# Zero-weight matmuls of 128 columns in the scan slots with little planned TensorE work

## The chip, the cores and the metric

The kernel runs on one core of one Trainium2 chip, as one program. The metric is device microseconds (us) for one execution. TensorE (PE), VectorE (DVE), ScalarE (ACT), GpSimd (POOL) and SyncE (SP) each work through an instruction list of their own and wait for one another through semaphores.

## The reference, cut to what matters

The input `x` is 16 images of 48x48 pixels with 96 channels. Two layers follow each other; each is a state-space block and then a quantized feed-forward block, both with a residual sum. The state-space block projects to 192 channels, convolves, and scans every image in four directions, with 16 states for every channel:

```python
# layer 0; layer 1 is alike, with a layer norm behind the scan
xs = cross_scan(silu(depthwise_conv(xc, conv_w, conv_b, 1)))
delta = softplus(dts @ dt_proj_w + dt_proj_b)
def step(h, inp):
    d_t, u_t, B_t, C_t = inp
    h = h * jnp.exp(d_t[..., None] * A) + (d_t * u_t)[..., None] * B_t[:, :, None, :]
    return (h, jnp.einsum('bkdn,bkn->bkd', h, C_t))
y = cross_merge(scan(step) + Ds * xs) * silu(z)
x = x + y @ out_proj_w.T + ...
x = x + ffn(norm(x))
```

## The kernel before, in words

The scans are the long part: 16 images by 2 layers give 32 scan phases. A phase has 288 steps (`STEPS`: two direction pairs, three chunks of 768 pixels, twelve row blocks and four state groups), so there are 9216 steps, and a step is one tile of 128 rows by 768 pixels. Each step passes through four engines:

- `decays` (L647, L651): ACT forms the decay factor `a` with an exponential, from `dl`, into PSUM. There are two such tiles.
- `added` (L656, L661): POOL multiplies `du` by `bs` for two steps at once, into one of eight `ring` tiles.
- `step` (L708): DVE runs the scan (L727). Then either DVE multiplies by `cs` (L729), or POOL does it later for two steps at once (`product`, L740); a running sum of planned microseconds in `self.load` decides which. ACT copies the last column to `carry` (L731).
- `folded` (L664): PE sums the states. A group of 16 steps has one PSUM tile `py` with two halves q (a pool with one buffer). At the group's first fold a matmul with `first` opens the sum in each half (L673); each fold then adds four matmuls of 32 output rows (L685), and the fold with g = 3 closes the sum. `stored` (L697, L700) has ACT copy `py` out.

Beside the scan of one image runs the other work of its neighbours: norms, projections, 3x3 convolutions as diagonal matmuls (L447), the gates, the output projections (L918, L948) and the feed-forward blocks. This work is written as generators. Each `yield` returns a planned weight, and the loop of `scans` (L754 to L784), which goes through the steps as slots, takes from the phase's generator (`todo`) as long as the weight given is below the phase's share. In a slot the order of emission is: loads, planned work, `stored`, `step`, `decays` of two steps ahead, `added` of four steps ahead, `product`, and at last the due folds. That order, written out by hand, is each engine's instruction list. Products of planned work go to `pst` tiles of 128x512 (`pst()`, two buffers), which ACT reads ("put") in a later stage of the pipeline `piped`, mostly one yield after the product.

So PE's list is a mixture of folds, which wait for DVE or POOL, and planned products, which wait for ACT to have freed a `pst` tile or to have written an input.

Of the kernel before, what the change touches and what calls it, by code (L numbers as in the profile page):

```python
# [13 lines left out]
F32 = mybir.dt.float32  # L14
# [19 lines left out]
ND = 32  # L34
NG = 4
GROUPS = NS // NG
STEPS = 2 * NCH * 12 * GROUPS
SPARE = 1.0


_P = np.arange(128)
# [7 lines left out]
class Pack:  # L49


    def __init__(self):
        self.at, self.n, self.parts = {}, 0, []
# [83 lines left out]
TQ = SUB // 128  # L137


class Net:  # L140
    def __init__(self, ctx, tc, wpack, at, b2, ffw):
        self.tc, self.nc = tc, tc.nc
        nc = self.nc
        pool = lambda name, **kw: ctx.enter_context(tc.tile_pool(name=name, **kw))
        self.const = pool("const", bufs=1)
# [42 lines left out]
            )  # L188
        self.ident16 = self.const.tile([128, 128], F16, name="ident16")
        nc.vector.tensor_copy(self.ident16, self.ident)  # L190
        self.ones16 = self.const.tile([128, 128], F16, name="ones16")
        nc.vector.memset(self.ones16, 0.0)
        nc.vector.memset(self.ones16[:1, :], 1.0)
# [34 lines left out]
        for v, name in (("g", "ong"), ("b", "onb")):  # L228
            for i, half in enumerate("ab"):
                n = (128, 64)[i]  # L230
                o = self.const.tile([128, DM], F32, name=f"ow{half}{v}")
# [357 lines left out]
    def scans(self, phases, rest):  # L589
# [3 lines left out]
        nc, tc = self.nc, self.tc  # L593
# [9 lines left out]
        total = [w for _, _, _, w in phases]  # L603
        given = [0.0] * len(phases)
        tiles = {w: {} for w in ("dl", "du", "b", "c")}
        firsts, cur, pys, ring = {}, {}, {}, {}
        folds, done = collections.deque(), []
        kept = {"carry": None, "before": None, "last": 0, "here": True, "product": None}

        def ready(f):  # L610
            assert f == 0 or todo[f - 1] is None, "what a scan reads is not written yet"
# [29 lines left out]
        def load_first(group):  # L641
            f, t, s, pair, c, j, i, g = steps[group * 4 * GROUPS]
            ready(f)
            firsts[group] = self.sw.tile([128, CH], F32, name="first", bufs=1)
            nc.sync.dma_start(firsts[group], s["u" if pair == 0 else "y"][j][:, c * CH : (c + 1) * CH])

        def decays(n):  # L647
            f, t, s, pair, c, j, i, g = steps[n]
            a = self.ps.tile([128, 2, 512], F32, name="a", tag="ps").rearrange("p q f -> p (q f)")[:, :CH]
            dl = tiles["dl"][n // 16, i // 2]  # L650
            nc.scalar.activation(a, dl[:, i % 2, :], AF.Exp, scale=rates[t][:, pair, j, i, g : g + 1])  # L651
            cur["a", n] = a
# [3 lines left out]
        def added(n):  # L656


            i = n % 4
            b = self.sw.tile([128, 2, CH], F32, name="ring", bufs=8)  # L660
            nc.gpsimd.tensor_tensor(b, tiles["du"][n // 16, i // 2], both(tiles["b"][n // 4]), ALU.mult)  # L661
            ring[n // 2] = b

        def folded(n, q):  # L664


            f, t, s, pair, c, j, i, g = steps[n]
            group = n // (4 * GROUPS)
            if (g, q) == (0, 0):
                pys[group] = self.psy.tile([128, 2, 512], F32, name="py")  # L670
            py = pys[group]
            if g == 0:
                nc.tensor.matmul(  # L673
                    py[:, q, :SUB],
                    lhsT=self.skip[t][:, j, :] if pair == 0 else self.ident,
                    rhs=firsts[group][:, q * SUB : (q + 1) * SUB],
                    start=True,
                    stop=False,
                )
                if q == 1:  # L680
                    del firsts[group]
                    if (group + 1) * 4 * GROUPS % STEPS:
                        load_first(group + 1)
            for k in range(4):
                nc.tensor.matmul(  # L685
                    py[32 * k : 32 * k + 32, q, :SUB],
                    lhsT=self.fold,
                    rhs=ring[(n + k) // 2][:, k % 2, q * SUB : (q + 1) * SUB],
                    start=False,
                    stop=(g == GROUPS - 1),  # L690
                )
            if q == 1:
                del ring[n // 2], ring[n // 2 + 1]
            if (g, q) == (GROUPS - 1, 1):
                done.append(group)

        def stored(group):  # L697
            f, t, s, pair, c, j, i, g = steps[group * 4 * GROUPS]
            yt = self.sw.tile([128, CH], F32, name="yt", bufs=1)
            nc.scalar.copy(sub(yt), pys.pop(group)[:, :, :SUB])  # L700
            to = s["y"][j][:, c * CH : (c + 1) * CH]
            if (pair, j) == (1, 1):
                for i in range(4):
                    nc.sync.dma_start(to.rearrange("(h r) f -> h r f", h=2)[:, 16 * i : 16 * i + 16], yt[32 * i : 32 * i + 32])
            else:
                nc.sync.dma_start(to, yt)

        def step(n):  # L708
            f, t, s, pair, c, j, i, g = steps[n]
            if (j, i, g) == (0, 0, 0):  # L710
                kept["before"] = kept["carry"] if c != (0, NCH - 1)[pair] else None
                kept["carry"] = self.sw.tile([128, 12 * GROUPS], F32, name="carry")
            way = (lambda ap: ap) if pair == 0 else (lambda ap: ap[:, ::-1])
            last = CH - 1 if pair == 0 else 0
            at = (4 * j + i) * GROUPS + g
            start = 0.0 if kept["before"] is None else kept["before"][:, at : at + 1]
            a, b, cc = cur.pop(("a", n)), ring[n // 2][:, n % 2, :], tiles["c"][n // 4]

            load = self.load
            if n % 2 == 0:  # L720
                load["gp"] = max(load["gp"], load["ve"] - 6.0)
                here = kept["here"] = load["gp"] + 2 * 3.42 > load["ve"] + 2 * 1.81 + SPARE
                load["gp"] += 3.42 if here else 2 * 3.42
                load["ve"] += 2 * 2.76 if here else 2 * 1.81
            here = kept["here"]
            h = a if here else b
            nc.vector.tensor_tensor_scan(way(h), way(a), way(b), start, ALU.mult, ALU.add)  # L727
            if here:
                nc.vector.tensor_tensor(b, h, cc, ALU.mult)  # L729
            if c != (NCH - 1, 0)[pair]:  # L730
                nc.scalar.copy(kept["carry"][:, at : at + 1], h[:, last : last + 1])  # L731
            kept["last"] = max(kept["last"], n + (1 if here else 4))
            if n % 4 == 3:
                at = max(n + 2, kept["last"])
                folds.extend([(at, n - 3, 0), (at + 1, n - 3, 1)])

        def product(n):

            b = ring[n // 2]
            nc.gpsimd.tensor_tensor(b, b, both(tiles["c"][n // 4]), ALU.mult)  # L740
# [13 lines left out]
        for n in range(-10, len(steps) + 10):  # L754
            for load, of_what in loads.pop(n, ()):
                load(*of_what)
            if (n + STEPS - EARLY) % STEPS == 0 and 0 <= n // STEPS + 1 < len(todo):
                ready(n // STEPS + 1)
                next(todo[n // STEPS + 1])
            if 0 <= n < len(steps):  # L760
                f = n // STEPS
                share = (n % STEPS + 1 - START) / (END - START)
                here = 0
                while todo[f] is not None and (share >= 1 or given[f] < total[f] * share - (here > 0)):
                    w = next(todo[f], "end")
                    if w == "end":
                        todo[f] = None
                    else:
                        given[f] += w
                        here += w  # L770
            if done:
                stored(done.pop())
            if 0 <= n < len(steps):
                step(n)
            if 0 <= n + 2 < len(steps):
                decays(n + 2)
            if n % 2 == 0 and 0 <= n + 4 < len(steps):
                added(n + 4)
            if n % 2 == 1:
                if kept["product"] is not None:  # L780
                    product(kept["product"])
                kept["product"] = n - 1 if 0 <= n < len(steps) and not kept["here"] else None
            while folds and folds[0][0] <= n and not (done and folds[0][1] % (4 * GROUPS) == 0):
                folded(*folds.popleft()[1:])  # L784
        assert not (folds or done or pys or loads)
        self.alone = True
        for _ in rest:
# [459 lines left out]
```

## Time and profile before

| | |
|---|---|
| time, median of 3 runs | 25081.68 us (25062.27 to 25085.71) |
| profiled execution: its own time | 25084.31 us |
| profiled execution: its span, first to last instruction | 25082.5 us |
| mean granted TensorE clock | 0.788 |
| PE busy, of which the weight load row | 16821.3 us (67%), PEld 7108.9 us (28%) |
| DVE busy | 22225.7 us (89%) |
| POOL busy | 22715.5 us (91%) |
| ACT busy | 15229.2 us (61%) |
| matmul records | 70912 |
| DMA | 5011.40 MB, 61.4% of the 16 engines' time on SyncE's queue |

A matmul of float32 operands stands in the trace as two records, each with a weight load: the program has 37472 matmuls, and the profile 70912 records. "PEclk" is the share of full TensorE clock that the throttle granted. In this trace it is either 1.0 or 0.5, in stretches that are multiples of 3.413 us. A row of a waits view reads: engine, what it was about to run, "<-", what it waited for, and then microseconds in total, number of times, and the longest. A row of groups reads: line, engine, operation, output <- inputs, shape, count, then busy time, mean ns of one, and idle time before them.

### The profile page before, as it was taken

How to read it: one execution, taken by the hardware profiler on the slowest of the kernel's cores; microseconds unless marked ns; L12 is line 12 of the kernel's file. 1: busy time of each engine (PE TensorE's matmuls, PEld its weight loads, DVE VectorE, ACT ScalarE, POOL GpSimd, SP SyncE). 2: the span in 40 equal slices, each digit the busy share in tenths (PEclk: the TensorE clock that was granted, in tenths of full speed). 3: DMA queues.
4: the chain of work that ended last, by engine and by line, in shares of the span. 5: the costliest groups of instructions: out<-in, count | busy, mean ns of one | idle time of the engine just before them, and what ended most of it. 6: DMA issues, size and time to landing. Idle time of an engine off the chain costs nothing. (4 is left out here: it accounts for less than half of the span.)

```text
span 25082.5 us, 233858 instructions
## 1 busy us (share of the span) xinstructions
PE 16821.3 (67%) x70912; PEld 7108.9 (28%) x70912; DVE 22225.7 (89%) x15758; ACT 15229.2 (61%) x26690; POOL 22715.5 (91%) x7372
## 2 busy tenths in 40 slices
PE   5667667666677666776666766667666676667765
PEld 2223223222232222332222322223222232223322
DVE  6888989888998898988998889998899888999887
ACT  4566656666556665666655666666666566666654
POOL 6999999999999899998999989999899998999997
PEclk7888778877788777887778877788777887778876
DMA  5666666665666666666666666566665666666664
GB/s 180 206 201 203 192 201 212 205 208 189 200 207 205 204 196 197 202 209 202 203 193 201 209 202 208 187 202 210 202 213 191 194 205 203 214 199 193 203 207 133
DMA packets 1898962, 5011.40 MB, mean 200 GB/s; under 512 B 348000, under 2 KB 348000, under 8 KB 1879008
## 3 DMA queue, kind: packets, MB, share of 16 engines
q1 hardware_dynamic: 1820576, 4952.35, 61.4%
q10 hardware_dynamic: 77120, 44.09, 0.6%
q8 instruction: 560, 9.18, 0.2%
q14 instruction: 706, 5.78, 0.1%
HBM read 4104.27 MB, written 891.22 MB: 199 GB/s over the span
## 5 line engine op out<-in xcount | busy, mean ns | idle before, releaser
L661 POOL TENSOR_TENSOR ring<-du,bs 128x1536 f32<-128x1536 f32 x4608 | 15768.7, 3445 | 761.7 <-DMA bs<-bc 394.4
L651 ACT ACTIVATE a<-dl,l_a 128x768 f32<-128x768 f32 x9216 | 8313.8, 904 | 3102.0 <-DVE ring L729 2263.9
L727 DVE TENSOR_TENSOR_SCAN a<-a,carry,ring 128x768 f32<-128x768 f32 x4054 | 7352.1, 1814 | 747.0 <-ACT a L651 679.1
L685 PE MATMUL py<-ring,fold_sb 128*32 128x384 f32 x36864 | 5212.3, 605 | 3041.7 <-POOL ring L740 2504.8
L740 POOL TENSOR_TENSOR ring<-ring,cs 128x1536 f32<-128x1536 f32 x1652 | 5687.4, 3443 | 823.3 <-issue 663.2
L729 DVE TENSOR_TENSOR ring<-a,cs 128x768 f32<-128x768 f32 x5912 | 5661.3, 958 | 463.5 <-DMA cs<-bc 71.0
L727 DVE TENSOR_TENSOR_SCAN ring<-a,carry,ring 128x768 f32<-128x768 f32 x2090 | 3691.8, 1801 | 362.0 <-ACT a L651 301.7
L727 DVE TENSOR_TENSOR_SCAN a<-a,ring 128x768 f32<-128x768 f32 x1858 | 3255.3, 1752 | 430.4 <-ACT a L651 367.9
L685 PEld LDWEIGHTS py<-ring,fold_sb 128*32 128x32 f32 x36864 | 1062.4, 122 | 6659.8 <-POOL ring L740 2964.4
L731 ACT COPY carry<-a 128x1 f32<-128x1 f32 x3778 | 600.1, 159 | 3723.5 <-DVE ring L729 3713.8
L727 DVE TENSOR_TENSOR_SCAN ring<-a,ring 128x768 f32<-128x768 f32 x1214 | 2069.8, 1740 | 193.0 <-ACT a L651 142.1
L339 PE MATMUL pst<-dts,wpack_sb 128*128 128x384 f32 x2304 | 1213.1, 665 | 1243.6 <-ACT dl L571 1217.2
L447 PE MATMUL pst<-e,dg 128*128 128x384 f32 x5184 | 1782.9, 493 | 0.0
L553 POOL TENSOR_TENSOR du<-dl,u 128x768 f32<-128x768 f32 x576 | 1042.6, 1820 | 564.2 <-DMA dd<-du 356.6
L447 PE MATMUL pst<-wxa,dg 128*128 128x384 f32 x3456 | 1220.9, 504 | 64.0 <-DMA dg<-taps_l1a 41.9
L447 PEld LDWEIGHTS pst<-e,dg 128*128 128x128 f32 x5184 | 945.9, 189 | 841.2 <-issue 214.4
L339 PE MATMUL pst<-xt,wpack_sb 96*128 96x384 f32 (+1 forms) x1536 | 766.5, 635 | 477.6 <-ACT wxb L482 261.2
L339 PEld LDWEIGHTS pst<-dts,wpack_sb 128*128 128x128 f32 x2304 | 512.6, 247 | 1929.3 <-ACT dl L571 1534.4
L673 PE MATMUL py<-first,l_skip 128*128 128x384 f32 x1152 | 655.5, 659 | 549.5 <-ACT yt L700 484.7
L339 PE MATMUL pst<-u,wpack_sb 128*128 128x384 f32 x2304 | 886.3, 531 | 190.8 <-ACT u L518 81.9
L673 PE MATMUL py<-first,ident 128*128 128x384 f32 x1152 | 631.8, 638 | 516.7 <-ACT yt L700 492.8
L339 PE MATMUL pst<-y,centre 128*128 128x384 f32 (+1 forms) x1536 | 819.3, 690 | 120.3 <-ACT y L969 114.8
(171 smaller groups left out, 17496.5 us busy)
## 6 DMA issues: line engine op xcount, KB each, us to landing
du<-dd SPq DMA_DIRECT2D x1536, 384.0 KB
dl<-dd SPq DMA_DIRECT2D x1536, 384.0 KB
bs<-bc SPq DMA_DIRECT2D x1536, 384.0 KB
cs<-bc SPq DMA_DIRECT2D x1536, 384.0 KB
du<-dd SPq DMA_DIRECT2D x1536, 192.0 KB
dl<-dd SPq DMA_DIRECT2D x1536, 192.0 KB
bs<-bc SPq DMA_DIRECT2D x1536, 192.0 KB
cs<-bc SPq DMA_DIRECT2D x1536, 192.0 KB
```

Source lines behind the costliest of these rows:

```text
L339: nc.tensor.matmul(img(o[: w.shape[1], :SUB]), lhsT=w, rhs=y, start=(k == 0), stop=(k == len(terms) - 1))
L447: nc.tensor.matmul(img(o[:, :SUB]), lhsT=dg[:n, k, :], rhs=img(p[:n], PW)[:, PQ * q + i : PQ * q + i + PQ, j : j + HW], start=(k == 0), st ...
L553: nc.gpsimd.tensor_tensor(du, dl[:, cs], u[j][:, cs], ALU.mult)
L651: nc.scalar.activation(a, dl[:, i % 2, :], AF.Exp, scale=rates[t][:, pair, j, i, g : g + 1])
L661: nc.gpsimd.tensor_tensor(b, tiles["du"][n // 16, i // 2], both(tiles["b"][n // 4]), ALU.mult)
L673: nc.tensor.matmul(py[:, q, :SUB], lhsT=self.skip[t][:, j, :] if pair == 0 else self.ident, rhs=firsts[group][:, q * SUB : (q + 1) * SUB], ...
L685: nc.tensor.matmul(py[32 * k : 32 * k + 32, q, :SUB], lhsT=self.fold, rhs=ring[(n + k) // 2][:, k % 2, q * SUB : (q + 1) * SUB], start=Fal ...
L727: nc.vector.tensor_tensor_scan(way(h), way(a), way(b), start, ALU.mult, ALU.add)
L729: nc.vector.tensor_tensor(b, h, cc, ALU.mult)
L731: nc.scalar.copy(kept["carry"][:, at : at + 1], h[:, last : last + 1])
L740: nc.gpsimd.tensor_tensor(b, b, both(tiles["c"][n // 4]), ALU.mult)
```

## The change

The builder keeps account of the TensorE time that it emits in a slot, and at the slot's end it adds matmuls with zero weights until the account reaches 1.2.

- A wrapper around `nc.tensor` (`Timed`, `Core`) adds to `spent` for every matmul: columns of the output times 4 for float32 (1 for other types), divided by 2400, and by 3 for the folds with 32 output rows.
- `spent` is set to zero in each slot ahead of the planned work.
- Behind the slot's folds `filled` forms n, the rounded (1.2 - spent) / 0.213, and emits n matmuls of 128 columns with the stationary operand `zero` (128x128, all zeros) and `ident` as the moving one.
- Where a sum of `py` is open (from the opening matmul to the fold with g = 3) they are added into its first 128 columns. Where none is open and the slot had no planned work, they go to a new `pst` tile named "fill". Otherwise none is emitted.
- One memset on DVE makes `zero`.

```diff
+FILL = 1.2
+class Timed:
...
+    def matmul(self, out, lhsT, rhs, **kw):
+        n = 1
+        for k in out.shape[1:]:
+            n *= k
+        self.spent[0] += n * (4 if rhs.dtype == F32 else 1) / 2400 / (3 if out.shape[0] == ND else 1)
+        return self.engine.matmul(out, lhsT=lhsT, rhs=rhs, **kw)
...
+        self.zero = self.const.tile([128, 128], F32, name="zero")
+        nc.vector.memset(self.zero, 0.0)
...
+            if g == 0:
+                begun[q] = py[:, q]
+            elif g == GROUPS - 1:
+                del begun[q]
             for k in range(4):
                 nc.tensor.matmul(
                     py[32 * k : 32 * k + 32, q, :SUB],
...
+        def filled(busy):
+
+            n = int((FILL - self.spent[0]) / 0.213 + 0.5)
+            if n <= 0:
+                return
+            if begun:
+                o, start = next(iter(begun.values()))[:, :128], False
+            elif not busy:
+                o, start = self.pst("fill")[:, :128], True
+            else:
+                return
+            for _ in range(n):
+                nc.tensor.matmul(o, lhsT=self.zero, rhs=self.ident, start=start, stop=start)
...
+            self.spent[0], here = 0.0, 0
             if 0 <= n < len(steps):
                 f = n // STEPS
                 share = (n % STEPS + 1 - START) / (END - START)
-                here = 0
...
             while folds and folds[0][0] <= n and not (done and folds[0][1] % (4 * GROUPS) == 0):
                 folded(*folds.popleft()[1:])
+            filled(here > 0)
```

More of the change, by code (lines that the diff above doesn't have):

```diff
@@ L137, with __init__, __getattr__ @@
 TQ = SUB // 128
+class Timed:
+    def __init__(self, engine, spent):
+        self.engine, self.spent = engine, spent
+    def __getattr__(self, name):
+        return getattr(self.engine, name)
+    def matmul(self, out, lhsT, rhs, **kw):
[4 more added lines that the diff above has]
+        return self.engine.matmul(out, lhsT=lhsT, rhs=rhs, **kw)
+class Core:
+    def __init__(self, nc, spent):
+        self.nc, self.tensor = nc, Timed(nc.tensor, spent)
+    def __getattr__(self, name):
+        return getattr(self.nc, name)
 class Net:
     def __init__(self, ctx, tc, wpack, at, b2, ffw):
-        self.tc, self.nc = tc, tc.nc
+        self.spent = [0.0]
+        self.tc, self.nc = tc, Core(tc.nc, self.spent)
         nc = self.nc
@@ L605, in scans @@
         tiles = {w: {} for w in ("dl", "du", "b", "c")}
-        firsts, cur, pys, ring = {}, {}, {}, {}
+        firsts, cur, pys, ring, begun = {}, {}, {}, {}, {}
         folds, done = collections.deque(), []
```

## The prediction

> **What bounds the kernel now.** I read the page's busy rows first, then the waits of DVE, ACT and PE, then PE's stretches at half clock.
>
> ```profile
> PE 16821.3 (67%) x70912; PEld 7108.9 (28%) x70912; DVE 22225.7 (89%) x15758; ACT 15229.2 (61%) x26690; POOL 22715.5 (91%) x7372
> ...
> PEclk7888778877788777887778877788777887778876
> ```
>
> DVE and POOL are near full, ACT and PE are not: the work of DVE and POOL is the floor, and PE counts only where it makes them wait. The page also says that the clock is low in every slice, 0.788 in the mean.
>
> ```profile
> DVE a L727 <- ACT a L651: 1047.0, 612, 7.4
> DVE ring L727 <- ACT a L651: 443.8, 281, 5.4
> ...
> ACT yt L700 <- PE py L685: 333.5, 194, 8.9
> ACT xs L953 <- PE pst L918: 289.1, 141, 3.9
> ACT y L969 <- PE pst L339: 259.2, 86, 5.0
> ...
> PE py L685 <- POOL ring L740: 2504.8, 452, 20.4
> PE pst L339 <- ACT dl L571: 1217.2, 217, 18.3
> ```
>
> The first two rows are how PE can reach the end: DVE's scan waits 1490.8 us (1047.0 + 443.8) for ACT's exponential, and ACT, which takes its list in order, may be late because a copy ahead of the exponential waited for PE. ACT's rows that wait for PE (sixteen of 30 us and more; three are shown) sum to 2045 us. Going through the idle times behind those 1490.8 us, and looking in the six us before each for an ACT wait for PE, I find 840 us so explained; in 244 of the 840 the granted clock was a half. The last two rows say why PE itself is late: its next matmul waits for POOL or ACT, up to 20 us, with planned work queued behind it.
>
> **What the clock follows.** Two pairs of neighbouring windows of the clock's 3.413 us grid (stretch, length, then busy time of PE, PEld, DVE, ACT and POOL, granted clock, DMA share, GB/s):
>
> ```profile
> 2619.35:2622.77 3.42, 3.42 (x24) 3.25 (x23) 3.42 (x4) 2.77 (x6) 3.42 (x2) 1.00 0.02 7
> 2622.77:2626.18 3.41, 3.41 (x13) 3.02 (x13) 3.32 (x4) 1.67 (x5) 3.41 (x2) 0.50 0.72 223
> ...
> 2639.83:2643.25 3.42, 1.35 (x6) 0.30 (x2) 3.38 (x3) 1.82 (x3) 3.42 (x2) 1.00 0.00 1
> 2643.25:2646.66 3.41, 1.65 (x6) 0.58 (x10) 2.32 (x3) 3.36 (x6) 3.41 (x2) 0.50 0.56 174
> ```
>
> In the third PE works 1.35 us of 3.42, and the next is at half clock. In the first PE is "busy" throughout, but with one-column matmuls (L984) whose time is weight loading; the next is at half clock too. So I counted the time in which columns stream, over all windows of the trace. Of 910 windows at full clock with columns streaming for under 0.37 of the window, 1% were followed by full clock; of 3309 above, 99%. At half clock the bound is 0.75 (1% below, 93% above): the same number of columns.
>
> **The change part by part.**
>
> *What is added.* The built program has 16103 fills behind 3964 of 9236 slots, mostly six (1959 slots, nothing planned) or two (1704 slots, one fold). The order on ACT, POOL and SP is unchanged, and DVE has one memset more at the start; that memset I cost at nothing, since DVE waits there for the weights' DMA. Nothing is removed.
>
> *What one fill costs.* No row has it. Two near ones:
>
> ```profile
> L447 PE MATMUL pst<-e,dg 128*128 128x384 f32 x5184 | 1782.9, 493 | 0.0
> ...
> L918 PE MATMUL pst<-wpack_sb,y 128*128 128x96 f32 x1152 | 199.5, 303 | 0.0
> ```
>
> Busy time over count is 0.344 us a record for the convolution at 384 columns, nearly all at full clock; a third of it, twice, is 0.229 us a fill. The 96-column row with the same weight load, over both clocks, gives 0.173 a record, 0.346 a fill. I take 0.28: 4.5 ms in all (3.7 to 5.6), against 8261 us in which PE is idle now.
>
> *What it does to the clock.* A slot is 2.72 us (25082.5 / 9216). Six fills stream for 1.28 us, 47% of it; two fills and a fold (0.64 us) for 39%. Paced by slots, that would be just over 0.37. But PE isn't paced by slots: fills carry no wait (215 wait for ACT and 118 for PE, the rest for nothing), so PE runs them as soon as it reaches them, then stands at the next fold or product as before. In PE's list they lie in 2723 runs, up to 26 or 32 long. They shorten idle times without pacing them, and where PE stands over one window behind a fold it still falls to half clock. I estimate 0.86 from laying the fills into the record (each starts when the matmul ahead of it ends): a third of the half-clock time goes.
>
> *The gain.* A third of the 244 us at half clock, halved: 41 us. Bounds: 0, and 146 us if all of PE's half-clock work (5949 us of its busy time) ran at full clock, by the rate below (2974 x 0.12 x 0.41). I take 50.
>
> *The loss.* Each fill stands ahead of the next fold or product in PE's list. 8593 stand ahead of folds, which wait now in any case (3041.7 us idle before L685, for POOL's product mostly): cover, and I cost them at nothing; without that cover they would come under the same rate. 7510 stand ahead of planned products (6558) or opening matmuls (952): 2.1 ms at 0.28. Now PE's 16821 us make ACT wait 2045, 0.12 per us, and 0.41 of that (840 of 2045) reaches DVE: 2.1 ms x 0.12 x 0.41 = 103 us. Lower end: 0, if all fall into idle time. Upper end: in the laid record, matmuls that stay where the trace shows them waiting but yield to the fills come 630 us later, in sum, than ACT's reads could bear (0.224 us a fill at full clock, 0.43 at half), 1131 us at 0.3 and 0.5; by 0.41 that is 258 or 464 us. Most is at the gates of the last stage (L830) and the third projection of the branch (L881, L883), where ACT follows close behind PE. I take 170, between the mean rate and the lower laid value, since DVE's own delays move the releases too.
>
> *Two small things.* A fill into a `pst` tile waits until ACT has read the tile's last product, and the next product then waits for the fill; products waiting for PE rise from 97 to 294, at 0.1 to 0.3 us each below 60 us, in the range. Inside a sum, two fills between a group's last two folds make `yt` some 0.5 us later where ACT waits for it (194 times, 333.5 us): counted in the loss.
>
> **Sum.** 25084.3 (the profiled execution's own time, 2.6 us above the median) + 170 - 50 = 25204, rounded 25205 us: slower by 0.5%.
>
> [...] The first window above is busy without a gap and loses the clock. [...]
>
> **The rivals.**
>
> *The fills fall into idle time* (27%). For it: 8261 us idle against 4.5 ms, the one slot of slack between a product and its read, and a DVE that waits for ACT more than for anything else. Against it: PE's lateness comes in bursts after a long wait, and the runs stand in just those bursts. Then only the gain is left, 50 to 146 us: 24980. This ends faster; it decides where a run's delay (6 x 0.28 = 1.7 us) stays below the 2.72 us of a slot.
>
> *Gain and loss cancel* (15%): each below 100 us, 25085, within 0.2%. That is about what a measurement of this kernel can tell from no change.
>
> *The clock doesn't move* (7%), because bursts leave the idle windows as they are or zero operands don't count as activity: the loss without the gain, 25255.
>
> *Backlog* (7%). In the last stage a slot pair has 2.56 us of centring products, folds and up to eight fills; at half clock eight fills take 3.4 of the pair's 5.4 us, PE no longer catches up, and 464 us are lost: 25550.
>
> **How the numbers follow.** My forecast, loss over gain, has 44%: 25205, of 25140 to 25400. Slower by over 0.2%: 44 + 7 + 7 = 58%; same 15%; faster 27%. The range runs from 24940 (the idle rival with nearly all of the gain) to 25480 (near the forecast's upper bound) and leaves out most of the backlog case and the best tail.
>
> **What would show it.** Right: a granted clock of 0.84 to 0.88, 16103 matmuls more (32206 records) at some 0.28 us, ACT's waits for PE up by some 400 us with L830 and L883 in front, and DVE's wait for ACT up by about 120. Wrong: ACT's waits for PE fall; then the fills were covered. A clock near 0.79 means the third rival; a clock over 0.93 means that pacing holds, and the gain is larger than I bound it.

## The result, and the profile after

The changed kernel takes 25327.58 us (median of 4, 25316.15 to 25333.9) against 25071.97 (median of 4): a ratio of 1.0101, 95% interval 1.0086 to 1.0117, or 256 us more. The profiled execution has a span of 25321.1 us and a granted clock of 0.872, after 0.788. The same lines of the page as for before:

```profile
PE 20054.1 (79%) x103118; PEld 10736.0 (42%) x103118; DVE 22188.8 (88%) x15759; ACT 15234.3 (60%) x26690; POOL 22747.1 (90%) x7372
...
PEclk8888889888888888888888988889888898888888
```

DVE, ACT and POOL have the same work, and their operations take as long as before (the exponential 904 ns before and 903 now, the scan that starts from `carry` 1814 in both). PE has 32206 records more, and no slice of its clock is below eight tenths, after 23 of 40 before. Yet DVE, whose span less busy time was 2856.8 us, now stands idle for 3132.3, or 275 us more: all of the difference is waiting. The waits of DVE and ACT in the changed kernel (microseconds, times, longest; the lines of the code moved down by 29 to 48, L774 is the scan, L680 the exponential, L1017 the copy of the centred product that was L969, and L154 is the wrapper through which all matmuls but the transposes now pass):

```profile
DVE a L774 <- ACT a L680: 1158.4, 628, 8.7
DVE ring L774 <- ACT a L680: 464.8, 285, 5.2
DVE ring L774 <- ACT carry L778: 150.5, 63, 10.4
...
ACT y L1017 <- PE pst L154: 411.6, 86, 12.0
ACT yt L747 <- PE py L154: 389.5, 187, 10.1
ACT xs L1001 <- PE pst L154: 341.1, 141, 4.7
...
PE py L154 <- POOL ring L787: 1311.1, 360, 18.3
PE pst L154 <- ACT dl L600: 851.8, 191, 11.4
PE fill L154 <- ACT y L1017: 81.0, 16, 10.9
```

DVE waits for the exponential 1623.2 us, 132 more than before. Over all of its rows it waits for ACT 2331.5 us after 2066.4, 265 more: the exponential is only half of the growth, and the copies of `carry` (74 us) and the root ahead of the reciprocal (26) are most of the rest. ACT waits more for PE: its rows that name PE, all of them, sum to 2545 us after 2173. The greatest growth is not where PE waits longest, but in one row: the centred products, 259.2 us before and 411.6 now. PE's own waits for POOL and ACT have shrunk (the two greatest rows from 2504.8 and 1217.2 us to 1311.1 and 851.8): fills stand in what was idle time, of which 5267.0 us are left of 8261.2.

Where in the run is the time? The starts of the 9216 scans give each phase's length. Of every four phases, the two with the last and the first stages in their planned work became 15.0 and 11.3 us longer (six phases of each kind in the middle of the run), the two with the middle stage 4.5 us longer and 0.2 us shorter. And within the first two kinds it is the first 48 of 288 steps. The table gives the mean of 13 such phases, in us for eight steps each; the last three rows belong to runs told below.

| run | 0-8 | 8-16 | 16-24 | 24-32 | 32-40 | 40-48 | sum |
|---|---|---|---|---|---|---|---|
| before | 22.5 | 21.4 | 25.8 | 23.5 | 17.8 | 20.5 | 131.7 |
| changed | 22.6 | 23.2 | 31.3 | 26.8 | 17.8 | 24.9 | 146.6 |
| no fills in centring | 22.5 | 21.5 | 25.7 | 23.4 | 17.8 | 20.1 | 131.1 |
| plain operands, before | 22.7 | 19.3 | 20.9 | 19.9 | 17.9 | 23.3 | 124.0 |
| plain operands, fills | 22.7 | 19.3 | 21.1 | 22.2 | 19.5 | 25.8 | 130.7 |

Fifteen such phases by 14.9 us are 224 us of the 256. These steps are `centred`: the centring products of layer 1 (steps 8 to 32), then 36 one-column matmuls for the sums of squares (L984 before) and the reciprocal on DVE (about 32 to 48). PE's order of time there, before, and then in the changed kernel (start, length, what ran, and the idle time ahead of it):

```profile
6411.81 8.14 PE L339 MATMUL pst<-y,centre 128*128 128x384 f32 x16
6419.87 0.85 PE L685 MATMUL py<-ring,fold_sb 128*32 128x384 f32 x8
6423.58 8.14 PE L339 MATMUL pst<-y,centre 128*128 128x384 f32 x16 [2.85 <-ACT y L969]
6431.65 1.50 PE L685 MATMUL py<-ring,fold_sb 128*32 128x384 f32 x16
6435.86 9.48 PE L339 MATMUL pst<-y,centre 128*128 128x384 f32 x16 [2.72 <-ACT y L969]
```

```profile
6475.11 8.04 PE L154 MATMUL pst<-y,centre 128*128 128x384 f32 x16
6483.07 0.85 PE L154 MATMUL py<-ring,fold_sb 128*32 128x384 f32 x8
6483.86 4.29 PE L154 MATMUL py<-ident,zero 128*128 128x128 f32 x36
6487.98 8.04 PE L154 MATMUL pst<-y,centre 128*128 128x384 f32 x16
6495.94 0.85 PE L154 MATMUL py<-ring,fold_sb 128*32 128x384 f32 x8
6496.73 0.71 PE L154 MATMUL py<-ident,zero 128*128 128x128 f32 x4
6497.37 0.85 PE L154 MATMUL py<-ring,fold_sb 128*32 128x384 f32 x8
6500.94 2.93 PE L154 MATMUL fill<-ident,zero 128*128 128x128 f32 x12 [2.72 <-ACT y L1017]
6503.93 9.49 PE L154 MATMUL pst<-y,centre 128*128 128x384 f32 x16
```

A pair of product rows stands in one slot, and the next pair about four slots, 10.9 us, later. The pair takes PE 8.14 us, and folds 0.85 to 1.7: 1 to 2 us are free. The builder's account puts the pair at 5.12 us, all in one slot, sees empty slots behind it and orders fills there: 18 behind the first pair shown (4.29 us), and 2 and 6 behind the second (0.71 and 2.93 us). Behind the first pair PE works on without a gap and still falls behind: 12.9 us to the next pair. Behind the second it stands 2.72 us ahead of the fills that take a `pst` tile, which ACT has yet to read, and the next pair comes 16.0 us after. Before it was 11.8 and 12.3. ACT's copy waits behind PE:

```profile
6477.89 0.47 ACT L1017 COPY y<-pst 64x384 f32<-64x384 f32 x1 [6.94 <-PE pst L154]
6478.26 0.19 ACT L778 COPY carry<-ring 128x1 f32<-128x1 f32 x1
6478.35 0.90 ACT L680 ACTIVATE a<-dl,l_a 128x768 f32<-128x768 f32 x1
```

The exponential, for which DVE's next scans wait, stands two places behind that copy.

### The profile page after: what moved, and what is told of

The parts are those of the page before. It is cut to its first block, busy times and chain, and to the rows that moved or that the text cites. A ratio compares the mean times of both kernels' runs of the same rounds, so it can differ in the third digit from the quotient of the medians.

```text
span 25321.1 us, 298313 instructions
## 1 busy us (share of the span) xinstructions
PE 20054.1 (79%) x103118; PEld 10736.0 (42%) x103118; DVE 22188.8 (88%) x15759; ACT 15234.3 (60%) x26690; POOL 22747.1 (90%) x7372
## 5 line engine op out<-in xcount | busy, mean ns | idle before, releaser
L680 ACT ACTIVATE a<-dl,l_a 128x768 f32<-128x768 f32 x9216 | 8312.5, 903 | 3048.7 <-DVE ring L776 2222.1
L774 DVE TENSOR_TENSOR_SCAN a<-a,carry,ring 128x768 f32<-128x768 f32 x4054 | 7354.3, 1814 | 771.9 <-ACT a L680 693.5
L154 PE MATMUL py<-ring,fold_sb 128*32 128x384 f32 x36864 | 4797.2, 562 | 1493.0 <-POOL ring L787 1311.1
L154 PEld LDWEIGHTS py<-ident,zero 128*128 128x128 f32 x28894 | 3722.0, 204 | 1717.1 <-issue 1673.3
L154 PE MATMUL py<-ident,zero 128*128 128x128 f32 x28894 | 4164.2, 297 | 0.0
L774 DVE TENSOR_TENSOR_SCAN ring<-a,carry,ring 128x768 f32<-128x768 f32 x2090 | 3691.9, 1801 | 357.5 <-ACT a L680 299.2
L774 DVE TENSOR_TENSOR_SCAN a<-a,ring 128x768 f32<-128x768 f32 x1858 | 3255.6, 1752 | 543.8 <-ACT a L680 464.9
L154 PEld LDWEIGHTS py<-ring,fold_sb 128*32 128x32 f32 x36864 | 865.4, 115 | 4027.1 <-issue 1775.9
L774 DVE TENSOR_TENSOR_SCAN ring<-a,ring 128x768 f32<-128x768 f32 x1214 | 2071.1, 1741 | 262.1 <-ACT a L680 165.6
L154 PE MATMUL pst<-dts,wpack_sb 128*128 128x384 f32 x2304 | 1143.6, 633 | 859.1 <-ACT dl L600 851.8
L154 PE MATMUL pst<-e,dg 128*128 128x384 f32 x5184 | 1779.9, 493 | 0.0
L154 PEld LDWEIGHTS pst<-e,dg 128*128 128x128 f32 x5184 | 946.0, 189 | 823.0 <-issue 198.8
L154 PE MATMUL pst<-wxa,dg 128*128 128x384 f32 x3456 | 1197.6, 495 | 36.9 <-DMA dg<-taps_l1a 20.3
L154 PEld LDWEIGHTS pst<-dts,wpack_sb 128*128 128x128 f32 x2304 | 497.0, 240 | 1391.0 <-ACT dl L600 1130.4
L154 PE MATMUL pst<-u,wpack_sb 128*128 128x384 f32 x2304 | 855.9, 517 | 118.7 <-ACT u L547 50.4
L154 PE MATMUL pst<-xt,wpack_sb 96*128 96x384 f32 (+1 forms) x1536 | 681.6, 574 | 297.0 <-ACT wxb L511 184.1
L154 PE MATMUL py<-first,l_skip 128*128 128x384 f32 x1152 | 613.0, 620 | 336.7 <-ACT yt L747 307.4
```

The lines of the kernel that those rows point to most:

```text
L154: return self.engine.matmul(out, lhsT=lhsT, rhs=rhs, **kw)
```

## The experiments

Theory A: all of the loss is PE's overfilled list in the centring stage. The first rivals are B, the mean rate of the prediction (every fill ahead of planned work costs alike), and C, the fills that take a `pst` tile. Later ones are D, that the clock is worth nothing, and E, that fills hurt in the stage for another reason than PE's time. Each time stands beside the kernel before on the same chip.

**Without the fills of the centring stage.** The flag is true from `loaded_y` in `centred` to behind the reciprocal.

```diff
+        self.centring = True
...
-            if n <= 0:
+            if n <= 0 or self.centring:
```

> The fills of the centring stage are left out (1738 of 16103, 11%); the other 14365 stay. Theory A, backlog in the centring stage: its strided products take PE 8.04 us of every four slots (10.9 us), so that fills there overfill PE; all of the loss is there. The time falls by 200 to 260 us, to between 25050 and 25130, DVE's waits for ACT fall back to about 1490 us, and the granted clock stays near 0.865. Theory B, the mean rate of the prediction (every fill ahead of a planned product costs alike): some 11 to 15% of the loss goes, 25290, and ACT's waits for PE stay above 2450 us.

25092.36 us, ratio 1.0012 (1.0003 to 1.0021), at a clock of 0.868.

```profile
DVE a L775 <- ACT a L681: 1061.2, 621, 7.4
DVE ring L775 <- ACT a L681: 456.5, 284, 5.4
...
ACT y L1019 <- PE pst L154: 258.9, 86, 4.9
```

The centred copies wait for PE as long as in the kernel before. Theory A holds and B falls: 11% of the fills carry nine tenths of the loss, and the other 14365 together cost 26 us, net of what the clock gives. ACT's rows that name PE sum to 2326 us, 153 more than before, and DVE stands idle for 55 us more (2911.4).

**Only these.**

```diff
-            if n <= 0:
+            if n <= 0 or not self.centring:
```

> The complement: only the 1738 fills of the centring stage. Theory A: slower than before by 200 to 250 us, 25280 to 25320, though the clock stays near 0.79. Theory B: by 30 to 40 us, 25105 to 25115.

25310.92 us, ratio 1.0097 (1.0083 to 1.0110), clock 0.795. The complement gives 244 us: the loss is there, and the clock is hardly touched by it. Here ACT's waits for PE grow by 237 us (to 2410) and DVE's idle time by 240 (to 3096.7): all of the lateness arrives at DVE. Two lines of its waits, which are almost those of the changed kernel:

```profile
DVE a L775 <- ACT a L681: 1159.1, 613, 8.6
...
ACT y L1019 <- PE pst L154: 418.9, 86, 11.7
```

**No fills into a tile of their own.**

```diff
-            elif not busy:
-                o, start = self.pst("fill")[:, :128], True
             else:
                 return
```

> The 1656 fills that take a pst tile are left out; the 14447 into open sums stay. Theory C, the tile: a fill that takes one of two pst tiles waits for ACT, and the next product waits for the fill, so that double buffering is lost; the loss goes with the tile, 25090 to 25150. Theory A: the fills into open sums overfill PE in the centring stage (1528 of its 1738), and at most 60 us come back, 25260 to 25320.

25258.45 us, ratio 1.0076 (1.0062 to 1.0090). Some 65 us come back (0.25%), a little over A's bound and far from C's: C holds for that part alone. The tile counts for about a quarter of the loss: in the centring stage a fill takes the tile that ACT has yet to read (the wait of 2.72 us in the order of time above), and PE stands there. The first 48 steps of a phase fit that: 141.4 us here, after 146.6 in the changed kernel.

**All fills with one column.**

```diff
-                nc.tensor.matmul(o, lhsT=self.zero, rhs=self.ident, start=start, stop=start)
+                nc.tensor.matmul(o[:, :1], lhsT=self.zero, rhs=self.ident[:, :1], start=start, stop=start)
```

> All 16103 fills, of one column instead of 128: about the same time of PE each (two weight loads, 0.27 us at full clock by the one-column rows of before) but hardly a column streamed. By the count of windows of before, the clock then stays near 0.78. Theory A with a clock that is worth some 50 us: 25370 to 25400, slower than the changed kernel by the worth of the clock. If weight loads count for the clock: 0.87 and 25330 as in the changed kernel. If the clock is worth nothing: 25330 at a clock of 0.78.

25826.63 us, ratio 1.0304 (1.0289 to 1.0318), clock 0.764: slower than the changed kernel by 499 us, not by the expected 50. The direction and the clock are A's, the size was wrong tenfold. The page's first line shows PE busy for longer than in the changed kernel, and yet at the lower clock:

```profile
PE 22162.9 (86%) x103118; PEld 12355.1 (48%) x103118; DVE 22216.4 (86%) x15759; ACT 15227.6 (59%) x26690; POOL 22737.3 (88%) x7372
```

So more weight loading didn't raise the clock here (PEld 7108.9 us at 0.788 in the kernel before, 12355.1 at 0.764), and columns of zero weights did (10736.0 at 0.872 in the changed kernel). The size has the centring stage in it (160.8 us for 48 steps after 146.6); the next run but one takes that out.

**Fills in the sparse phases alone.**

```diff
+            if n <= 0 or self.centring:
...
-            filled(here > 0)
+            if n // STEPS % 4 in (0, 3):
+                filled(here > 0)
```

> Fills only in the phases whose planned work is that of a last and a first stage (two of every four, with little of it), and none in the centring stage: 8283 fills. With the centring stage left out those phases were 2.4 to 2.8 us shorter each than before, 16 of them, and the others longer by 1 to 4 us. Theory A with a clock that is worth something where PE has little to do: 25025 to 25045 beside a before of 25067, faster by 0.1 to 0.2%. Theory D, the clock is worth nothing and the phases moved by chance: 25060 to 25085.

25054.06 us, ratio 0.9998 (0.9989 to 1.0007), clock 0.835. No difference from before that can be measured: neither theory is confirmed.

**One column, none in the centring stage.** Both edits above together.

> As the run without fills in the centring stage (25092), but each fill is of one column. The same 14365 fills in the same places, hardly a column streamed. Theory A with a clock that pays for the queue time of the fills: outside the centring stage the one-column kernel was some 35 us longer in every four phases than the changed one, so about 25370, at a clock near 0.77. Theory D, clock worth nothing: 25090 to 25120 at a clock near 0.77.

25335.99 us, ratio 1.0110 (1.0095 to 1.0126), clock 0.770. With 128 columns the same list took 25092, at a clock of 0.868: 244 us of difference, where D expected 25090 to 25120, so D falls. The first line of both pages, and the rows of the fills into open sums, first with 128 columns and then with one:

```profile
PE 19664.4 (78%) x99642; PEld 10338.8 (41%) x99642; DVE 22186.0 (88%) x15759; ACT 15228.1 (61%) x26690; POOL 22738.7 (91%) x7372
...
L154 PE MATMUL py<-ident,zero 128*128 128x128 f32 x25838 | 3714.6, 296 | 0.0
```

```profile
PE 21505.3 (85%) x99642; PEld 11722.4 (46%) x99642; DVE 22195.6 (88%) x15759; ACT 15232.0 (60%) x26690; POOL 22737.3 (90%) x7372
...
L154 PE MATMUL py<-ident,zero 128*128 128x1 f32 x25838 | 4365.3, 295 | 0.0
```

Busy time over count is 0.144 and 0.169 us a record: a one-column fill isn't shorter, but longer. From start to start, a 128-column fill of the changed kernel takes 0.112 us a record at full clock and 0.213 at half, and a one-column record of the kernel before (L984) 0.132 and 0.235; how much of the greater length comes from the lower clock isn't shown. PE is busy for 1841 us more, of which 651 are these rows; the row of the folds, for one, grew from 4806.2 to 5251.7 us. So the 244 us hold both the fills' own greater length and longer planned work and folds; how they divide, this run doesn't tell.

**Plain operands in the centring stage, kernel before.**

```diff
-    def loaded_y(self, s):
+    def loaded_y(self, s, plain=False):
...
-        turned = lambda yj: lambda q: swapped(yj)[:, q * PQ : (q + 1) * PQ]
+        turned = lambda yj: same(yj) if plain else lambda q: swapped(yj)[:, q * PQ : (q + 1) * PQ]
...
-        xt, y, *parts = yield from self.loaded_y(s)
+        xt, y, *parts = yield from self.loaded_y(s, True)
```

> The kernel before, but in the centring stage the two operands that are read with a stride of a row (the turned pixels) are read plainly instead; this leaves out the turning there, so what is computed differs. A pair of product rows then takes PE some 5.2 us of every four slots instead of 8.04. Reference for the next run: 24870 to 25000, since the stage makes DVE wait less.

24922.8 us, ratio 0.9943 (0.9929 to 0.9957). The stage's rows, first in the kernel before, then in this one:

```profile
L339 PE MATMUL pst<-y,centre 128*64 128x384 f32 x768 | 392.3, 659 | 0.0
```

```profile
L339 PE MATMUL pst<-y,centre 128*64 128x384 f32 x768 | 269.4, 494 | 0.0
```

0.511 us a record with half of the operands read at a stride, 0.351 with none. In the kernel before, from start to start at full clock, a record of these products takes 0.644 us where its operand is strided and 0.323 where it isn't. The builder's account knows no stride.

**Plain operands with the fills.** The same edit in the changed kernel.

> The changed kernel with the same plain operands in the centring stage, all 16103 fills. Theory A, PE's time in the stage is what overflows: 5.2 us of products, 1.7 of folds and 3 to 4 of fills fit into 10.9, and the loss against the kernel before with plain operands falls from 255 to at most 90 us. Theory E, the fills hurt there for another reason (their place ahead of the products, the tile): 200 to 260 us over that kernel.

25045.38 us, ratio 0.9991 (0.9982 to 1.0000): 123 us over the run before it, between A's bound of 90 and E's range. The table of steps above tells why. In steps 8 to 24, the products, the loss is gone (0.2 us). What stays is 6.4 us of a phase in steps 24 to 48, some 96 us over the fifteen (with the 26 us of the fills elsewhere that is the 123): the end of the products and the one-column matmuls, whose time is mostly weight loading (224.1 of 231.3 us in the changed kernel) and which plain operands don't help. In the changed kernel such a stretch reads (length, busy time of PE, PEld, DVE, ACT, POOL, granted clock, DMA):

```profile
6549.85:6573.12 23.27, 23.27 (x98) 15.75 (x97) 15.91 (x13) 9.40 (x17) 19.83 (x6) 0.53 0.63 217
```

PE has no gap, at nearly half clock, and DVE's reciprocal comes after it:

```profile
6572.10 0.27 DVE L1045 RECIPROCAL rt<-rt 128x18 f32<-128x18 f32 x1 [7.10 <-ACT rt L1043]
```

So A holds for the products, where the loss goes with PE's time. For the one-column matmuls, the second place where PE is full, it is argued from the steps and from this stretch; no run leaves out the fills there alone.

**Spread product rows, kernel before.** The pair of rows is emitted one yield apart, in the same order.

```diff
-        for weights in zip(*halves):
-            yield from weights
+        for _ in range(NQ + 1):
+            for half in halves:
+                yield next(half)
```

> The kernel before with one edit: in the centring stage the two product rows of a pair (128 and 64 channels), which it emits in one slot, are emitted one yield apart, in the same order. Theory A says that the stage is short of PE time in a burst: ACT's copy waits behind 8.04 us of products and then DVE behind ACT. Spread, ACT's wait for the centred products falls from 259 us to under 150 and the time by 50 to 120 us, 24950 to 25020. If only the total of PE's time counts, nothing changes: 25050 to 25080.

24969.07 us, ratio 0.9956 (0.9942 to 0.9970). ACT's wait at these copies, 259.2 us before, is now:

```profile
ACT y L969 <- PE pst L339: 113.0, 74, 4.6
```

The stage's burst was a cost of the kernel before already, and this is the better version's main part.

**Spread rows with all fills.** The same edit in the changed kernel.

> The changed kernel with the same spreading, some 300 fills fewer. If the burst makes the fills dear: at most 150 us over the spread kernel before. If PE's total in the stage does (8.04 us of products, 1.7 of folds, 3 to 4 of fills in 10.9): still 180 to 260 us over it.

25178.82 us, ratio 1.0038 (1.0024 to 1.0052): 210 us over the spread kernel before, where it was 256 without spreading. It is PE's total in the stage that overflows, and the burst is the smaller part.

**More fill.** `FILL = 2.0`, none in the centring stage.

> FILL = 2.0 in place of 1.2, none in the centring stage: 28027 fills, nearly twice the 14365 of that kernel. Theory A: the clock rises to 0.93 or more, PE's lists lengthen by 3.9 ms, and the loss outside the centring stage outgrows the clock's worth: 25150 to 25350. If the clock is worth more than the queue time: below 25067.

25280.09 us, ratio 1.0081 (1.0067 to 1.0095), clock 0.920: 0.7% (some 175 us) over 1.2, for 13662 fills more. The clock rose a little less than expected, and more clock doesn't pay for the longer list.

**Spread rows, fills in the sparse phases.**

> Spread centring, fills only in the two sparse phases of every four and none in the centring stage. Within 30 us of the spread kernel before if fills outside the centring stage are worth nothing; 15 to 45 us below it if the clock's worth in those phases is real.

24948.25 us, ratio 0.9946 (0.9933 to 0.9958), clock 0.837. It beats both kernels, by 0.5% and 1.5%. Its interval overlaps that of the spread kernel without fills (0.9942 to 0.9970); 21 us here and 14 us in the other pair point one way, but that these fills gain anything isn't shown.

## Why the prediction was right and wrong

- *The side and the range held*: slower, 25328 within 24940 to 25480. The size was half: 120 us forecast, 256 measured. That the range held is in part luck: the numbers that made it wide came from lateness at the gates and the branch's projection, and the loss was elsewhere.
- *The price of a fill* held: 0.28 us taken, 0.288 measured (4164.2 us over 28894 records, twice).
- *The clock* held: 0.86 estimated, 0.872 measured. The columns' bound held with it: the same count over the changed kernel's trace finds 851 windows at full clock with columns streaming for under 0.37, of which 2% were followed by full clock, and 4658 above, of which 99% were. The rival of a clock that doesn't move falls.
- *The cover* is shown only net: 8593 fills ahead of folds and the rest outside one stage cost 26 us together, after what the clock gave. PE's waits before folds for POOL fell from 2504.8 to 1311.1 us.
- *The gain*, 50 us, stays open. PE's matmuls without the fills are busy for 15.4 to 15.9 ms after 16.8 (the span between the two is time in which fills and others overlap); by the prediction's own rate, 0.12 x 0.41, that is worth 46 to 70 us. The 244 us against the list without columns are for another step of the clock, 0.770 to 0.868, and have the fills' own length in them. How much the clock gave and queue time took within the 26 us, no run tells apart.
- *The loss* is the step that failed, in place and in size. I spread 7510 fills by a mean rate and looked for the lateness at the gates and the branch's projection (L830, L883): those grew by 21 us (two rows, 103.2 to 124.1) and 56 us (74.2 to 130.4), the centred copies by 152. The mean rate says nothing of a stage that is full. 1738 fills in it cost 244 us, 0.14 us each; 14365 elsewhere 26 net.
- *The share that reaches DVE*, 0.41, was the mis-sized factor. ACT's waits for PE grew by 372 us (some 400 were forecast), but DVE's idle time by 275, that is 0.74. The two complementary runs show why: with the fills of the centring stage alone ACT waits 237 us more for PE and DVE stands idle 240 more, all of it; without them 153 and 55, a share of 0.36 (net of the clock's gain), near what was taken. New lateness in this full stage found no slack to vanish in. The share also counted waits for the exponential alone, and these did grow nearly as forecast (132 us, some 120 forecast); all of DVE's waits for ACT grew by 265.
- *The rival of backlog* had the mechanism and the stage, at 7% and 464 us. It failed in two numbers. It put the two rows at 2.56 us of a slot pair, 5.12 in four slots, by the builder's account, where the trace has 8.04 to 8.14 us in four slots. And it expected half clock and 0.43 us a fill, where the clock was 0.94 in the mean (steps 8 to 40 of the 13 phases) and a fill cost some 0.28.
- *The two small things*, below 60 us: the fills in tiles of their own were worth some 65 us.

## What to carry to other kernels

A filler on an engine that takes its list in order can cost next to nothing, net, over most of a program (26 us for 14365 here) and half of its own length in a stage where that engine is already full (0.14 us each for 1738). So look for the stage in which ACT's copies wait for PE, and not at the engine's idle share. An account of planned time must be set against the trace's records stage by stage: here one form of operand took twice its planned time (0.644 us a record, and 0.323 without the stride), and the account started anew in each slot, so that the slots behind a burst looked empty. And the clock that rose from 0.788 to 0.872 showed here only that more columns streamed: the time rose with it, by 256 us.

## What the runs showed of the hardware

Matmuls with zero weights raised the clock: 14365 of them with 128 columns from 0.788 to 0.868, while with one column it was 0.770, at PE busy for longer (21505.3 us after 19664.4). PE's idle time didn't decide it: 8261.2 us stand beside a clock of 0.788 in the kernel before, 5267.0 beside 0.872 in the changed kernel, and in the run with all fills of one column only 3668.7, beside 0.764, the lowest of the three. So in these runs the clock went with the columns that streamed, and not with PE's idle time. A moving operand read with a row's stride took 0.644 us a record of 384 columns at full clock in the kernel before, and 0.323 without.
